# Nine z buffers, other operation estimates and a longer patience with ScalarE's tables, in a planned scan, attention and mixture kernel

## Chip, cores and metric

One core of a Trainium2 chip runs the whole kernel. The metric is the device time of one execution in microseconds, the median of several runs. The five engines are named as in the profile: PE (TensorE), DVE (VectorE), ACT (ScalarE), POOL (GpSimd) and SP (SyncE, which issues nearly all DMAs).

## What is computed

The input is `x` of shape (4, 384, 32, 32), all float32. The reference has two layers, cut here to what matters.

```python
# layer 0: group norm, then a selective scan in four directions
xs = cross_scan(gn(x))                                  # rows, columns, and both reversed
dts, Bs, Cs = split(einsum('bkdl,kcd->bkcl', xs, x_proj_weight), [12, 16, 16])
dt = softplus(einsum('bkrl,kdr->bkdl', dts, dt_projs_weight) + dt_projs_bias)
# per batch, direction, channel d and state n, along 1024 places:
h = h * exp(dt * A) + (dt * u) * B
y = sum over n of h * C
x = x + gelu(layernorm(cross_merge(y + D * u)))
# layer 1: per batch 1024 tokens of 384
t = t + attention(ln(t))          # 6 heads of 64, causal, 64 keys back
t = t + mixture(ln(t))            # 4 experts, the best 2 of each token, hidden size 1536, gelu
```

## The kernel before

**The scan.** One tile holds 128 rows of 1024 places: 32 channels by 4 of the 16 states. A block is 32 channels of one direction of one batch (192 blocks), and each has 4 such groups of states, so there are 768 scan slots. Two blocks make a pair whose slots alternate: slots 8p to 8p+7 belong to pair p, even slots to its first block and odd ones to its second (`place_of`). A slot is five steps.

- `times_b` (L808): POOL multiplies the spread dt*u (a dtu tile) by B into a z buffer. It may be up to three slots ahead of the scan (AHEAD, L547).
- `decay` (L824): ACT makes dA = exp(dt * A) from the spread dt (a dts tile) into one of two PSUM buffers.
- `scan` (L850): one DVE instruction runs the recurrence, in place in z or in dA.
- `times_c` (L837): the product by C, by POOL from z into z, or by DVE from dA into z. The choice is made in `scan` by the planned clocks of the two engines, and POOL is chosen only when z is three slots ahead.
- `fold_y` (L884): PE adds up the states by products with a constant matrix into a PSUM bank, two slots at a time. Then those two z buffers are free, and after four such steps DVE adds the bank to the earlier directions' sum, which SP loads from and stores to device memory.

`time_steps` makes dt and dt*u of a third of a direction (exp and ln on ACT, products on DVE) and writes them to device memory as dtr. `spread` (L798) loads them back, block by block and with every channel repeated four times, into the dts and dtu tiles; in the profile both loads are named dts<-dtr. A block's dtu tile is released after its fourth `times_b`, its dts tile after its fourth `decay`. `group_norm` (L618) prepares the next batch; from the z buffers it takes one for each yd tile and two at once for xo.

**The rest.** Attention of a batch (`tokens`) starts when the scan of that batch is folded. Then come its routing and its experts. Experts work in blocks of 128 rows, 19 per batch and 76 in all; a block has four chunks, each of which is a product into one PSUM bank (`hidden`, L1350), three gelu instructions on ACT (`gelus`, L1371) and a product into the output. Three banks (`banks`) serve folds, attention and `hidden` together. Eight weight buffers serve attention, which keeps four of them, and the experts.

**What sets the order.** Nothing of the order is written out by hand. Every part is a Python generator that yields the operation it wants next, and class `Machine` keeps a planned clock for each engine. An operation gets an estimated cost in `Engine.ask` (L154). `Machine.choose` (L322) takes, for each engine, an operation that is ready at the planned time, and the program's order on each engine is the order of these choices. On the chip every engine runs its list in that order and waits by semaphores, so an instruction that is not ready holds up all behind it. An estimate changes no instruction, only the order.

For ACT, `choose` prefers operations that need no other activation table than the loaded one. An operation of another table is taken when it has been ready for longer than PATIENCE, or when nothing else is ready. `settled` (L257) delays a request until its inputs are planned to be written by half a microsecond from now (SOON).

Of the kernel before, what the change touches and what calls it, by code (L numbers as in the profile page):

```python
# [17 lines left out]
P = 128  # L18
B, D, HH, WW = 4, 384, 32, 32
L = HH * WW  # L20
# [22 lines left out]
HID_RANK = 2  # L43
GELU_BIAS = EARLY
FAVOUR = 1.0
TILES, EPS, NZ = 3, 1e-5, 7
CORES = 1
NEG = -1.0e30

# [80 lines left out]
class Engine:  # L130
# [23 lines left out]
    def ask(self, op, a, k):  # L154
        aps = [v for v in list(a) + [v for n, v in k.items() if n not in ("out", "accum_out")] if hasattr(v, "tensor")]
        if "out" in k:
            outs, ins = [k["out"]], aps
        else:
            outs, ins = aps[:1], aps[1:]
        if op == "value_load":  # L160
            outs, ins = [], aps
        if op == "tensor_tensor_reduce":
            outs, ins = outs + ins[-1:], ins[:-1]
        if k.get("accum_out") is not None:
            outs = outs + [k["accum_out"]]
        for v in list(k.values()):
            if isinstance(v, bass.IndirectOffsetOnAxis):
                ins = ins + [v.ap]
        n = max(v.free_size() if callable(v.free_size) else v.free_size for v in (outs if op == "matmul" else outs + ins))
        size, table = 0, None  # L170
        if "dma" in op:
            size = max(_nbytes(v) for v in outs + ins[:1])
            if op == "indirect_dma_start":
                size = P * D * 4
            cost = dict(pool=1.0, act=0.38, sp=0.48)[self.name]
        elif self.name == "pe":
            cost = max(n, 122) * (0.00088 if op == "transpose" else 0.00176)
            if outs[0].shape[0] == 32:
                cost = 0.01 + 0.00022 * n
            if ins[0].shape[0] < 32:  # L180
                cost *= 0.6
        elif self.name == "act":
            cost = 0.08 + 0.00085 * n + 0.1 * sum(hasattr(k.get(v), "tensor") for v in ("bias", "scale"))
            cost += 0.19 if "accum_out" in k else 0.0
            table = TABLES.get(a[2]) if op == "activation" else None
        elif self.name == "pool":
            cost = 0.1 + 0.0022 * n
        elif self.name == "sp":
            cost = 1.5
        else:  # L190
            cost = 0.17 + 0.00198 * n if "scan" in op else 0.14 + 0.00105 * n
            if n < 256 and not any(v.space == PSUM for v in outs + ins):
                cost += 0.5
        asked = Op(self.name, outs, ins, cost, table, size)
        if self.name == "pe":
            asked.work = cost * min(ins[0].shape[0], P) / P if outs[0].shape[0] > 32 else 0.5 * cost
        return asked


def _nbytes(ap):  # L200
    n = 4
    for s in ap.shape:
        n *= s
    return n
# [6 lines left out]
class Machine:  # L211
# [42 lines left out]
            t = max(t, r + (HOP if e != eng else 0.0))  # L254
        return t

    def settled(self, *tiles):  # L257

        names = [ap.tensor.name for ap in tiles]
        return lambda: max(self.written.get(n, (0.0, None))[0] for n in names) <= self.t + SOON  # L260

    def account(self, op, start):
        e = op.eng
# [58 lines left out]
    def choose(self, eng):  # L322
# [4 lines left out]
        if eng == "act":  # L327

            same = [p for p in able if p[2].table in (None, self.table)]
            late = [p for p in able if p[2].table not in (None, self.table) and t0 - p[0] > PATIENCE]  # L330
            able = late or same or able
# [34 lines left out]
            raise RuntimeError("tracing is stuck")  # L366


PATIENCE = 3.0
SOON = 0.5  # L370
WINDOW, COLD = 3.413, 1.9
MARGIN, QUEUES = 1.0, ("sp",)

# [3 lines left out]
def conv_attn_hybrid(  # L377
# [89 lines left out]
    m = Machine(nc)  # L467
# [41 lines left out]
    work = ctx.enter_context(tc.tile_pool(name="work", bufs=1))  # L509
    rp = ctx.enter_context(tc.tile_pool(name="rp", bufs=2))  # L510
    zs_ = Stock(m, work, "z", NZ, [P, L])
    dtus, dts = (Stock(m, work, n, 4, [P, L]) for n in ("dtu", "dts"))
    bs_, cs_ = (Stock(m, work, n, 4, [P, L]) for n in ("rb", "rc"))
    rows = Stock(m, work, "row", NROW, [P, D])
    xbs, xbts, hss, ybs = (
# [38 lines left out]
    def place_of(s):  # L554

        return s // SP * 2 + s % 2, s % SP // 2
# [280 lines left out]
    def times_c(s, h, on_pool):  # L837
        n, g = place_of(s)
        i = blocks[n][0]
        yield lambda: (i, g, 1) in bcs  # L840
        if on_pool:
            yield from pool.tensor_tensor(zs[s], zs[s], bcs[i, g, 1], ALU.mult)
        else:
            yield from dve.tensor_tensor(zs[s], h, bcs[i, g, 1], ALU.mult)
            das_.give(h)
        if n % NB == NB - 1:
            cs_.give(bcs.pop((i, g, 1)))
        ready.add(s)

    def scan():  # L850

        for s in range(NSLOT):
            n, g = place_of(s)
            i = blocks[n][0]
            yield lambda: s in zs and s in das
            z, da = zs[s], das.pop(s)
            on_pool = count_of["times"] >= min(s + AHEAD, NSLOT) and m.clock["pool"] < m.clock["dve"] + LEAD
            h = z if on_pool else da
            if turns[i][1] >= 2:
                yield from dve.tensor_tensor_scan(  # L860
                    h[:, ::-1], da[:, ::-1], z[:, ::-1], 0.0, ALU.mult, ALU.add
                )
            else:
                yield from dve.tensor_tensor_scan(h, da, z, 0.0, ALU.mult, ALU.add)
            count_of["scan"] = s + 1
            if s % SP == 0:
                m.spawn(fold_y(n), EARLY)
            if on_pool:
                das_.give(da)
                m.spawn(times_c(s, h, True))  # L870
            else:
                yield from times_c(s, h, False)
        ended.append(True)
        yield lambda: len(das_.free) == 2
        for stock in (banks, ybank):
            stock.free.append(das_.free.pop(0))
        for stock, n in ((zs_, NZ), (dts, 4), (dtus, 4)):
            yield lambda: len(stock.free) == n
            rows.free += stock.free
            stock.free = []  # L880
# [3 lines left out]
    def fold_y(n):  # L884


        i, t, j = blocks[n]
        b, k = turns[i]
        rows_y = ydr[b][t, j : j + 2].rearrange("j r l -> (j r) l")
        prev = yield from yps.take("yp")  # L890
        yield from sp.dma_start(prev, rows_y)
        ps = None
        for g in range(NG):
            s = n // 2 * SP + 2 * g
            yield lambda: s in ready and s + 1 in ready
            pair = zs[s], zs[s + 1]
            yield m.settled(*pair)
            mm = Calls()
            if ps is None:
                ps = yield from banks.take("ps_y", 0)  # L900
            for n_z, z in enumerate(pair):
                for h in range(2):
                    if k % 2:
                        rhs = z.rearrange("p (w h) -> p w h", h=HH)[:, :, ts(h, HH // 2)]
                    else:
                        rhs = z[:, ts(h, LH)]
                    q = 32 * (2 * n_z + h)
                    mm.matmul(ps[q : q + 32, :], fold, rhs, start=g == 0, stop=g == NG - 1)
            yield from pe.all(mm)
            zs_.give(zs.pop(s), zs.pop(s + 1))  # L910
        yield from dve.tensor_tensor(prev, ps, prev, ALU.add)
        if k == LAST_BY_COLUMNS:
            yield from act.copy(
                ps.rearrange("p (h w) -> p w h", w=WW), prev.rearrange("p (w h) -> p w h", w=WW)
            )
            yield from act.copy(prev, ps)
        banks.give(ps)
        yield from sp.dma_start(rows_y, prev)
        yps.give(prev)
        folded[b] = folded.get(b, 0) + 2  # L920
        if folded[b] == KG * NB:
            have.add(("scan", b))
# [553 lines left out]
    with tc.manual_schedule():  # L1476
        for b in range(B):
            m.spawn(group_norm(b), EARLY)
        for gen in (turn_loads(), time_steps(), state_rows(0), state_rows(1), spread(1), spread(0)):
            m.spawn(gen, EARLY)  # L1480
        for gen in (decay(), times_b(), scan()):
            m.spawn(gen)
        m.spawn(layer1(), EARLY)
        for gen in (prepare(), mixture()):
            m.spawn(gen, LATER)
        m.run()
# [54 lines left out]
```

## Time and profile before

| | |
|---|---|
| runs | 4070.57, 4078.01, 4080.30 us; median 4078.01 |
| profiled execution | 4065.49 us, of it the span from first to last instruction 4063.8 |
| busy, of the span | PE 74%, DVE 71%, ACT 60%, POOL 70% |
| scan on DVE | 768 instructions, 2.276 to 2.288 us each on average |
| product by B on POOL | 768, 2.358 us each |
| product by C | 375 on POOL at 2.356 us, 393 on DVE at 1.221 us |
| dA on ACT | 768, 1.116 us each |
| activation tables | 388 loads, 1.283 us each |
| mean granted TensorE clock | 0.804 of full speed |

Times in the profile are microseconds unless marked ns. In a group of instructions, the numbers after the first bar are their busy time and the mean length of one in ns; those after the second bar are the idle time of the engine just before them, and what ended it. In a list of waits the numbers are the total, how many, and the longest. L141 and L152 are the two helper lines through which all planned operations go, so groups are told apart by the names of their tiles. [...]

### The profile page before, as it was taken

Reading aid. Unit: us, or ns where it says so; the run is one execution under the profiler, and the core shown is the slowest. Engines: PE = TensorE matmul, PEld = TensorE weight load, DVE = VectorE, ACT = ScalarE, POOL = GpSimd, SP = SyncE. Lnnn points to the kernel's source line nnn. Section 1 sums busy time; section 2 is a strip of 40 time slices with the busy share of each in tenths; the row PEclk is TensorE's granted clock in tenths of the full one; section 3 lists DMA queues with packets and bytes.
Section 4 is the critical chain, followed back from the end, with each engine's and each line's share of the span. In section 5 each row is a group of like instructions: output and inputs, shape, how many; then the busy total and the mean of one; then the engine's idle time right before and its main releaser. Section 6 shows DMA issues by size and latency. Waiting matters only on the chain. (4 is left out here: it accounts for less than half of the span.)

```text
span 4063.8 us, 49234 instructions
## 1 busy us (share of the span) xinstructions
PE 3014.8 (74%) x15856; PEld 1854.0 (46%) x15856; DVE 2878.0 (71%) x3064; ACT 2432.7 (60%) x3979; POOL 2855.7 (70%) x1490
## 2 busy tenths in 40 slices
PE   3554455576674888677777786767799999998998
PEld 1000000043441455445454444444466788887886
DVE  2999999998889888888888889888897232101001
ACT  3554455476774798777776787877777345222221
POOL 1999989989897789999987899899997110101001
PEclk8555566577775899878877787887799999998997
DMA  5565564634345989464668795664569754998995
GB/s 200 203 250 209 217 209 151 209 109 162 114 154 184 382 315 355 164 229 140 215 209 283 268 358 195 230 197 171 190 243 337 240 170 142 345 335 295 315 317 193
DMA packets 368570, 935.11 MB, mean 230 GB/s; under 512 B 48372, under 2 KB 160120, under 8 KB 368312
## 3 DMA queue, kind: packets, MB, share of 16 engines
q1 hardware_dynamic: 360120, 906.79, 63.6%
q0 software_dynamic: 8192, 25.17, 1.8%
q8 instruction: 126, 2.06, 0.2%
q14 instruction: 132, 1.08, 0.1%
HBM read 786.39 MB, written 164.30 MB: 234 GB/s over the span
## 5 line engine op out<-in xcount | busy, mean ns | idle before, releaser
L141 POOL TENSOR_TENSOR z<-dts,bc 128x1024 f32<-128x1024 f32 x768 | 1792.2, 2358 | 177.7 <-PE ps_y L152 95.3
L141 ACT ACTIVATE dA<-dts,a 128x1024 f32<-128x1024 f32 x768 | 851.1, 1116 | 485.5 <-DVE z L141 456.6
L152 PE MATMUL ps_y<-z,fold 128*32 128x512 f32 x3072 | 734.9, 806 | 536.1 <-POOL z L141 253.6
L141 DVE TENSOR_TENSOR_SCAN dA<-dA,z 128x1024 f32<-128x1024 f32 x393 | 899.1, 2288 | 107.6 <-ACT dA L141 88.6
L141 POOL TENSOR_TENSOR z<-z,bc 128x1024 f32<-128x1024 f32 x375 | 879.6, 2356 | 102.6 <-DVE z L141 99.7
L141 DVE TENSOR_TENSOR_SCAN z<-dA,z 128x1024 f32<-128x1024 f32 x375 | 843.8, 2276 | 41.2 <-ACT dA L141 39.4
L152 PEld LDWEIGHTS ps_hid<-xbt,w_sb 128*128 128x128 f32 x5472 | 682.1, 201 | 132.5 <-issue 25.7
L152 PE MATMUL ps_hid<-xbt,w_sb 128*128 128x128 f32 x5472 | 702.0, 286 | 38.0 <-ACT dt L141 19.4
L152 PE MATMUL y_ff<-w_sb,hs 128*128 128x384 f32 x1824 | 659.7, 500 | 19.2 <-ACT hs L141 15.2
L141 ACT ACTIVATE hs<-ps_hid,bb 128x128 f32<-128x128 f32 x912 | 270.5, 366 | 457.1 <-PE ps_hid L152 351.6
L152 PEld LDWEIGHTS ps_y<-z,fold 128*32 128x32 f32 x3072 | 95.1, 123 | 971.4 <-POOL z L141 466.2
L141 ACT ACT_TABLE_LOAD x388 | 497.8, 1283 | 17.2 <-issue 3.6
L141 DVE TENSOR_TENSOR z<-dA,bc 128x1024 f32<-128x1024 f32 x393 | 479.8, 1221 | 13.0
L152 PEld LDWEIGHTS y_ff<-w_sb,hs 128*128 128x128 f32 x1824 | 331.7, 195 | 240.5 <-issue 47.5
L141 POOL DMA_INDIRECT cb<-ysdr,idx x64 | 61.7, 963 | 441.6 <-issue 281.7
L141 DVE COPY xbt<-ps_xb 128x384 f32<-128x384 f32 x39 | 21.7, 556 | 407.7 <-PE ps_xb L152 407.7
L152 POOL TENSOR_TENSOR rn<-rn,half 128x1 f32<-128x1 f32 x96 | 52.5, 547 | 265.6 <-DVE rn L152 256.2
L141 POOL DMA_INDIRECT xsdr<-tks,idx x64 | 63.9, 999 | 168.9 <-DMA xsdr<-tks,idx 119.5
L152 PE MATMUL ps_dt<-xd,dtw_sb 12*128 12x512 f32 x192 | 99.8, 856 | 45.9 <-ACT dt L141 19.2
L152 PE MATMUL ps_o<-v,pt 128*128 128x64 f32 (+1 forms) x720 | 110.1, 315 | 19.6 <-DVE tt L141 7.2
L141 ACT COPY dt<-ps_sp 128x512 f32<-128x512 f32 x96 | 56.0, 584 | 113.5 <-DVE e L141 113.2
L152 PEld LDWEIGHTS ps_o<-v,pt 128*128 128x128 f32 (+1 forms) x720 | 104.9, 227 | 29.4 <-DVE tt L141 7.7
(189 smaller groups left out, 3219.4 us busy)
## 6 DMA issues: line engine op xcount, KB each, us to landing
w_sb<-wl SPq DMA_DIRECT2D x608, 576.0 KB
dts<-dtr SPq DMA_DIRECT2D x384, 512.0 KB
bc<-xdr SPq DMA_DIRECT2D x128, 512.0 KB
ub<-udr SPq DMA_DIRECT2D x48, 512.0 KB
dtr<-e SPq DMA_DIRECT2D x48, 512.0 KB
dtr<-dt SPq DMA_DIRECT2D x48, 512.0 KB
yp<-ydr SPq DMA_DIRECT2D x96, 256.0 KB
ydr<-yp SPq DMA_DIRECT2D x96, 256.0 KB
```

The lines of the kernel that those rows point to most:

```text
L141: return getattr(self.real, op)(*a, **k)
L152: getattr(self.real, op)(*a, **k)
```

## The change

Five things change; the instructions that compute are the same.

- There are nine z buffers, not seven, and three dtu and three dts buffers, not four of each. All are 128 x 1024 tiles, fifteen before and after.
- The estimates for folds, for products with fewer than 32 rows and for ACT are larger. The share of a fold's cost that counts for the planned clock of TensorE is larger too.
- PATIENCE is 5.0, not 3.0.
- The constant SOON is replaced by an argument of `settled`, whose default is -0.5.
- `fold_y` passes SURE, which is -0.5, as that argument.

```diff
-TILES, EPS, NZ = 3, 1e-5, 7
+TILES, EPS, NZ, SURE = 3, 1e-5, 9, -0.5
...
             if outs[0].shape[0] == 32:
-                cost = 0.01 + 0.00022 * n
+                cost = 0.02 + 0.0004 * n
             if ins[0].shape[0] < 32:
-                cost *= 0.6
+                cost *= 0.9
         elif self.name == "act":
-            cost = 0.08 + 0.00085 * n + 0.1 * sum(hasattr(k.get(v), "tensor") for v in ("bias", "scale"))
+            cost = 0.1 + 0.00088 * n + 0.1 * sum(hasattr(k.get(v), "tensor") for v in ("bias", "scale"))
...
-            asked.work = cost * min(ins[0].shape[0], P) / P if outs[0].shape[0] > 32 else 0.5 * cost
+            asked.work = cost * min(ins[0].shape[0], P) / P if outs[0].shape[0] > 32 else 0.7 * cost
...
-    def settled(self, *tiles):
+    def settled(self, *tiles, sure=-0.5):
...
-        return lambda: max(self.written.get(n, (0.0, None))[0] for n in names) <= self.t + SOON
+        return lambda: max(self.written.get(n, (0.0, None))[0] for n in names) <= self.t - sure
...
-PATIENCE = 3.0
-SOON = 0.5
+PATIENCE = 5.0
...
-    dtus, dts = (Stock(m, work, n, 4, [P, L]) for n in ("dtu", "dts"))
+    dtus, dts = (Stock(m, work, n, 3, [P, L]) for n in ("dtu", "dts"))
...
-        for stock, n in ((zs_, NZ), (dts, 4), (dtus, 4)):
+        for stock, n in ((zs_, NZ), (dts, 3), (dtus, 3)):
...
-            yield m.settled(*pair)
+            yield m.settled(*pair, sure=SURE)
```

## The prediction

> **What bounds the kernel now.** I read the page's 40 slices first (one slice is 101.6 us), then busy time by stretch, then the waits of each engine, then the groups.
>
> ```profile
> span 4063.8 us, 49234 instructions
> ...
> PE   3554455576674888677777786767799999998998
> ...
> DVE  2999999998889888888888889888897232101001
> ACT  3554455476774798777776787877777345222221
> POOL 1999989989897789999987899899997110101001
> ```
> For 31 slices DVE and POOL are at 8 to 9 tenths: the loop over 768 scan slots, from its first scan at 104 us to its last at 3140. For the rest PE alone is full. So the time is the loop's length plus the PE work left when the loop ends.
>
> ```profile
> 800.00:1300.00 500.00, 330.46 (x1638) 189.92 (x1638) 435.79 (x539) 330.05 (x559) 442.05 (x238) 0.70 0.41 142
> 1300.00:1600.00 300.00, 239.52 (x1337) 147.75 (x1337) 256.14 (x172) 251.38 (x341) 258.09 (x116) 0.89 0.92 345
> 1600.00:2200.00 600.00, 451.43 (x2393) 282.57 (x2392) 512.97 (x548) 458.43 (x731) 540.10 (x275) 0.82 0.61 208
> 3500.00:4064.00 564.00, 532.73 (x3185) 428.42 (x3183) 37.68 (x72) 130.61 (x413) 44.68 (x47) 0.94 0.86 301
> ```
> The columns are stretch, length, then busy us of PE, its weight loads, DVE, ACT, POOL, then clock, DMA share, GB/s. Summed over the six stretches that make up 800 to 3145, DVE is busy 2041 and POOL 2097 of 2345 us: idle 304 and 248. From 100 to 800 they idle only 26 and 39 of 700, so nothing is to be had there.
>
> The gelu groups count expert blocks (12 gelus each): 35 blocks run under the loop, 41 after it. At 3800 to 4000, 150 gelus are 12.5 blocks: **16 us a block** in the tail. Under the loop the pace is 98 gelus in 1400 to 1600, 4.1 blocks per 100 us, while no attention runs, and 75 in 1600 to 2200 and 84 in 2400 to 3000, 1.1 per 100 us, while it does.
>
> ```profile
> POOL z L141 <- DVE z L141: 99.7, 44, 13.3
> POOL z L141 <- PE ps_y L152: 95.3, 50, 10.0
> ...
> DVE dA L141 <- ACT dA L141: 88.6, 68, 3.8
> ...
> DVE z L141 <- ACT dA L141: 39.4, 35, 3.6
> ...
> DVE dA L141 <- POOL z L141: 12.5, 9, 6.3
> ```
> These are us in total, times, longest. POOL waits for a z buffer that a fold on PE must free (95.3), yet DVE hardly waits for POOL (12.5): its waits are for ScalarE's dA (128.0).
>
> **The change, part by part.** The scheduler is a model run while the program is written; its costs alter only the order on each engine.
>
> *Nine z buffers.* A fold frees two every two slots. Two slots are 2 x 3.96 us (3036 us / 767 steps) = 7.9 us, so two more buffers cover a fold that is late by 7.9 us; the 50 waits average 1.9 us, the longest is 10.0. I take the whole 95.3 us, and 10.0 us of waits on xdr<-xo (xo holds z buffers), off POOL: 105 us. It shortens the loop only if the order then gives POOL more products by C. One moved product costs POOL 2.356 us and saves DVE 1.221, so w us freed on POOL give w x 1.221/3.577 = 0.341 w: **-36 us**. Ends: 0 (DVE waited 12.5 in all) and -105. What is late next on POOL is the product by C behind its scan (99.7) and the spread loads.
>
> *Three dtu and three dts buffers.* Blocks go in pairs. With three buffers, the pair's second block waits until the pair before has finished its first: released at slot 6, needed at slot 9. In this trace that gap is 4.6 to 17.4 us on POOL (5th to 90th percentile, median 10.2) and 6.8 to 15.3 on ACT (median 10.0). A load's landing, read as its semaphore's last update before that semaphore's next use, comes 3.3 to 12.5 us after issue (median 4.9) and up to 16.7 after the release. Laid against each other pair by pair, 10 of 93 loads come late for POOL by 31 us in all and 7 for ACT by 13. POOL's converts as above, ACT's in full: 31 x 0.341 + 13 = 24. What hides it is the lead of z (median 6.0 us before its scan) and of dA (2.0): I take half, **+12 us**. Ends: 0, and 44 if every gap shrank to its lower quartile (6.9 and 8.1: 60 and 23 us late). SP issues at the same releases as before, so nothing queued behind these loads moves.
>
> The Trainium skill, "DMA: Bandwidth & Descriptors", section "Anatomy of one DMA — SWDGE (gpsimd) path", gives about 2.0 us plus bytes/436e9 for the GpSimd path. As an estimate for 512 KB that is 3.2 us, and no load would be late; this trace's quickest load agrees at 3.3, its median of 4.9 does not, and the sum goes by the trace.
>
> *PATIENCE 3 to 5.*
>
> ```profile
> L141 ACT ACTIVATE dA<-dts,a 128x1024 f32<-128x1024 f32 x768 | 851.1, 1116 | 485.5 <-DVE z L141 456.6
> ...
> L141 ACT ACT_TABLE_LOAD x388 | 497.8, 1283 | 17.2 <-issue 3.6
> ```
> 388 loads at 1.283 us, 368 of them before 3145. But `choose` waits only if an operation of the loaded table, or of none, is ready; an idle ScalarE changes tables at once, and it idles 485.5 us before dA. In the trace 112 stretches under the loop hold only expert gelus; 80 of them hold one chunk. I take a tenth of 368 away: 37 loads, 47 us of ScalarE. DVE waited 92.6 us for a dA with a load just before it, so a tenth is **-9 us**. Ends: -93 and +93, since longer gelu stretches delay a dA too. The other side: a ps_hid chunk can hold one of three PSUM banks 2 us longer. I take half a block lost to the tail, +8 us (ends: 0 and +94, worked out below).
>
> ```profile
> 2605.01 0.47 ACT L141 COPY yb<-y_ff 128x384 f32<-128x384 f32 x1
> ...
> 2605.51 1.28 ACT L141 ACT_TABLE_LOAD   x1
> ...
> 2606.80 0.37 ACT L141 ACTIVATE hs<-ps_hid,bb 128x128 f32<-128x128 f32 x1
> ```
> The load follows the copy by 0.03 us and the gelu follows the load by 0.01. The Trainium skill, "ScalarE: Activation LUTs", section "What ACT_TABLE_LOAD costs", adds a drain of about 1380 ns, 2.66 us a switch. At that price 37 loads would be 98 us of ScalarE instead of 47; this trace shows no drain, so 1.283 is used.
>
> *Estimates.* A fold product goes from 0.123 to 0.225 us warm; the trace has 734.9 us for 1536 calls (two of the 3072 records each), 0.478. A 12-row time-step product goes from 0.541 to 0.811 (99.8 us for 96 calls, 1.040). An exp goes from 1.050 to 1.101 (trace 1.116), a gelu from 0.289 to 0.313 (0.366). PE was planned too fast and its folds came late. What a truer order can touch is POOL's 99.7 us behind scans (x 0.341 = 34) and DVE's waits on PE from 800 to 3145, 106.7: 141. I take a third, **-48 us**; ends -141 and +141, for a new order can also be a worse one.
>
> *SURE.* -0.5 makes `t - sure` the old `t + 0.5`: nothing.
>
> **The sum.** Loop: -36 + 12 - 9 - 48 = -81 us. A shorter loop leaves more expert blocks to the tail: between 81 x 0.011 x 16 = 14 and 81 x 0.041 x 16 = 53 us; middle 34. With the half block: -81 + 34 + 8 = -39. The profiled execution took 4065.5 us (span 4063.8), so 4026.5 by it; the median of the three runs shown, 4078.0, is 12.5 above it, so **4039**.
>
> **The rivals.** *More.* Half the idle of DVE and POOL goes (276 / 2 = 138 us), tail given back at the middle rate (0.42): -80, 3998. For it: both engines idle 11 to 13%. Against it: DVE's waits are scattered over many small causes.
>
> *Nothing.* The z waits were harmless (DVE waited 12.5 us), the loads go on as before since ScalarE is idle when it switches, and late spreads cost 12 x 0.58 = 7: 4085.
>
> *Slower.* Longer-held PSUM banks starve the experts. In 1300 to 1600, 2200 to 2400 and 3000 to 3145 (645 us) 21.9 blocks run, a chunk each 7.4 us; at 2 us more it is 69 chunks instead of 88, 4.7 blocks or 76 us of tail, and 1.1 blocks, 18 us, more in the attention stretches: 94. Against a net loop gain of 47: +47, 4125. It decides from about 3 lost blocks (47 / 16). For it: a fold keeps one bank throughout. Against it: patience only counts while exp work is queued.
>
> **How the numbers follow.** The smallest difference a measurement can tell is about 0.3%, 12 us. Forecast 4039 (its own range 3998 to 4066): 0.40. More: 0.18. Nothing: 0.14. Slower: 0.28. Faster is 0.58. Range 3960 to 4135: down past the second case, since the ends of the order term allow it, up past the slower one.
>
> **What would show it.** Right: POOL's waits on ps_y near 0; the last scan near 3060; 43 blocks after it; 340 to 360 table loads; few POOL or ACT waits on dts<-dtr. Wrong: waits on dts<-dtr over 60 us (late spreads); 45 or more blocks after the loop at an unchanged loop (banks); loads still near 388 and loop unchanged (nothing); more waits of DVE on PE or ACT than 107 and 128 (a worse order).

## The result, and the profile after

The changed kernel takes 4105.72 us (median of four runs, 4102.83 to 4107.63) and the kernel before 4074.29 us beside it (4065.28 to 4080.30). The ratio is 1.0077, with a 95% interval from 1.0063 to 1.0090: slower by 31 us. The profiled execution took 4107.63 us, of it a span of 4105.9.

First the 40 slices of the changed kernel (one is now 102.6 us), and the groups of the product by B and of the table loads.

```profile
span 4105.9 us, 49117 instructions
...
PE   3544444467766497777777778777899999998998
...
DVE  2999999999898888998988688999882233101001
ACT  3545455477675588777777687777772344222221
POOL 1999989999998899999987899999991110001001
...
L141 POOL TENSOR_TENSOR z<-dts,bc 128x1024 f32<-128x1024 f32 x768 | 1794.0, 2359 | 127.3 <-DMA dts<-dtr 88.3
...
L141 ACT ACT_TABLE_LOAD x338 | 433.7, 1283 | 15.4 <-PE ps_hid L152 4.8
```
DVE and POOL leave the high digits about one slice earlier, and 50 of the 388 table loads are gone. In the waits of POOL and DVE (total, times, longest), the wait for a fold fell from 95.3 to 34.4 us. A wait for late spread loads came in its place; 68.8 of its 88.3 us are the very first load, which was 67.3 of 69.4 before, so the other loads rose from 2.1 to 19.5 us. ScalarE too now waits for a spread load before a dA, 10 times and 27.5 us in all, where in the kernel before it never did.

```profile
POOL z L141 <- DMA dts<-dtr: 88.3, 9, 68.8
POOL z L141 <- DVE z L141: 67.0, 32, 8.6
...
POOL z L141 <- PE ps_y L152: 34.4, 6, 17.1
...
DVE dA L141 <- ACT dA L141: 83.9, 56, 6.3
...
DVE z L141 <- ACT dA L141: 38.6, 29, 3.4
```
The loop's last scan ends at 3082 us, 58 earlier than in the kernel before. Yet the span is 42 longer, so the stretch after the loop grew by 100. Two answers of the windows view, for the instructions on the hs tiles alone, show why. The ACT column counts gelus, 12 to a block. This is the kernel before, cut at its loop's end:

```profile
800.00:3140.00 2340.00, 310.08 (x831) 154.92 (x832) 125.26 (x420) 0.81 0.64 226
3140.00:4064.00 924.00, 349.65 (x995) 176.78 (x993) 145.24 (x493) 0.96 0.76 262
```
And this is the changed one, cut at its own:

```profile
800.00:3082.00 2282.00, 269.21 (x711) 133.84 (x712) 105.77 (x357) 0.79 0.63 219
3082.00:4106.00 1024.00, 393.88 (x1114) 198.79 (x1112) 164.25 (x555) 0.96 0.77 269
```
Of the 912 gelus, 493 fell after the loop before (41.0 blocks) and 555 do now (46.2). At 16 us a block, 5.2 blocks are 83 of the 100 us. So the loop became shorter, by 58 us where 81 were forecast, and the tail took back 83 us where 42 (34 + 8) were forecast.

### The profile page after: what moved, and what is told of

It reads as the page before. It is cut to its first block, busy times and chain, and to the rows that moved or that the text cites. A ratio compares the mean times of both kernels' runs of the same rounds, so it can differ in the third digit from the quotient of the medians.

```text
span 4105.9 us, 49117 instructions
## 1 busy us (share of the span) xinstructions
PE 3060.7 (75%) x15868; PEld 1885.7 (46%) x15868; DVE 2884.5 (70%) x3062; ACT 2359.8 (57%) x3914; POOL 2884.8 (70%) x1503
## 5 line engine op out<-in xcount | busy, mean ns | idle before, releaser
L141 POOL TENSOR_TENSOR z<-dts,bc 128x1024 f32<-128x1024 f32 x768 | 1794.0, 2359 | 127.3 <-DMA dts<-dtr 88.3
L141 POOL TENSOR_TENSOR z<-z,bc 128x1024 f32<-128x1024 f32 x388 | 911.9, 2357 | 74.9 <-DVE z L141 67.0
L141 DVE TENSOR_TENSOR_SCAN dA<-dA,z 128x1024 f32<-128x1024 f32 x380 | 869.3, 2288 | 95.3 <-ACT dA L141 83.9
L141 DVE TENSOR_TENSOR_SCAN z<-dA,z 128x1024 f32<-128x1024 f32 x388 | 872.4, 2276 | 47.0 <-ACT dA L141 38.6
L141 DVE TENSOR_TENSOR z<-dA,bc 128x1024 f32<-128x1024 f32 x380 | 464.0, 1221 | 11.1
L152 PE MATMUL ps_s<-k,q 64*128 64x192 f32 (+1 forms) x384 | 101.5, 408 | 53.3 <-ACT dt L141 27.5
L141 DVE COPY yb<-y_ff 128x384 f32<-128x384 f32 x29 | 16.0, 553 | 177.0 <-PE y_ff L152 146.6
```

Source lines behind the costliest of these rows:

```text
L141: return getattr(self.real, op)(*a, **k)
L152: getattr(self.real, op)(*a, **k)
```

## Experiments

Three theories were put against each other. **A**: the larger estimates cost the time. **B**: the longer patience does, by way of the PSUM banks. **C**: any new order moves the time by some tens of microseconds, and what was measured is mostly that. Times are medians; the kernel before, run beside each group, gave 4073.8 to 4079.8. Blocks left are expert blocks whose gelus come after the last scan, and the loop's end is the end of that scan, both from the profiled execution of each run.

### The parts alone

**e1, the buffers alone.**

```diff
-TILES, EPS, NZ = 3, 1e-5, 7
+TILES, EPS, NZ = 3, 1e-5, 9
...
-    dtus, dts = (Stock(m, work, n, 4, [P, L]) for n in ("dtu", "dts"))
+    dtus, dts = (Stock(m, work, n, 3, [P, L]) for n in ("dtu", "dts"))
```


> The kernel before with nine z and three dtu and dts buffers alone. Theory A (the larger estimates cost the time: with them the order gives attention and the experts less of PE under the loop, and 5 blocks of 16 us more are left for the tail): this run lacks them, the loop is 30 to 60 us shorter, at most 2 blocks more than 41 are left, 10 to 35 us faster than before. Theory B (patience: a chunk's gelus hold a PSUM bank longer): the same as A here. Theory C (any new order moves the time by some tens of us, and no part has an effect of its own): anywhere within 30 us of before. Late spread loads would show as over 60 us of waits on dts<-dtr and no gain.

Measured: 4090.8 us, ratio 1.0022 (1.0009 to 1.0036). The loop ends at 3136, 42.8 blocks are left, 347 table loads. POOL's waits for folds fall to 7.0 us, and its waits for spread loads behind the very first are 25.2. Neither A's gain nor the 60 us of late loads.

**e2, the patience alone.**

```diff
-PATIENCE = 3.0
+PATIENCE = 5.0
```


> The kernel before with PATIENCE 5 alone. Theory A: table loads fall to 340 to 370, blocks left after the loop stay within 1.5 of 41, time between 30 us faster and 10 slower. Theory B: 44 or more blocks are left after the loop, 30 to 90 us slower than before. Theory C: within 30 us of before, loads alone follow the setting.

Measured: 4089.5 us, ratio 1.0026 (1.0012 to 1.0041), 358 loads, 41.2 blocks left. B finds no support here: no block is lost. In the trace a chunk's first gelu under the loop starts 1.6 us after its last product on average, and 1.7 before, so the banks are not held longer.

**e3, the estimates alone.**

```diff
-                cost = 0.01 + 0.00022 * n
+                cost = 0.02 + 0.0004 * n
...
-                cost *= 0.6
+                cost *= 0.9
...
-            cost = 0.08 + 0.00085 * n + 0.1 * sum(hasattr(k.get(v), "tensor") for v in ("bias", "scale"))
+            cost = 0.1 + 0.00088 * n + 0.1 * sum(hasattr(k.get(v), "tensor") for v in ("bias", "scale"))
...
-            asked.work = cost * min(ins[0].shape[0], P) / P if outs[0].shape[0] > 32 else 0.5 * cost
+            asked.work = cost * min(ins[0].shape[0], P) / P if outs[0].shape[0] > 32 else 0.7 * cost
```


> The kernel before with the new estimates alone (folds, 12-row products, ScalarE). Theory A: attention of the first three batches takes longer by tens of us each, 45 to 49 blocks are left after the loop instead of 41, 50 to 120 us slower than before. Theory B: no block is lost, within 20 us of before. Theory C: within 30 us of before.

Measured: 4147.5 us, ratio 1.0163 (1.0142 to 1.0184). The loop ends at 3078, and 48.8 blocks are left.

**e4, buffers and patience, no estimates** (the edits of e1 and e2).

> The change without its estimates: nine z buffers and PATIENCE 5. Theory A: keeps the shorter loop (3075 to 3110) and loses at most 2 blocks, 15 to 60 us faster than before and 45 to 90 faster than the whole change. Theory B: still 44 or more blocks left, slower than before by 10 to 50. Theory C: within 30 us of before.

Measured: 4036.3 us, ratio 0.9887 (0.9867 to 0.9908), faster than both kernels. The same windows as above, for e4:

```profile
800.00:3094.00 2294.00, 288.62 (x798) 142.86 (x798) 118.75 (x405) 0.80 0.65 228
3094.00:4034.00 940.00, 362.22 (x1026) 182.75 (x1026) 149.82 (x507) 0.96 0.77 264
```
The loop is 47 us shorter than before, and only 507 gelus (42.2 blocks) are left. With or without buffers and patience the estimates cost about 70 us (4147.5 against the 4079.8 of the kernel before beside it, 4105.7 against 4036.3). That fits A. But against the same 4079.8 buffers and patience lose 11 and 10 us alone and gain 44 together, which no sum of effects gives. So C had to be measured.

### What chance in the order is worth

HOP is the planned time of a handover between engines. Two thousandths of a microsecond mean nothing, but they decide near ties another way, and every later choice may follow.

```diff
-HOP = 0.15
+HOP = 0.148
```
Likewise 0.149, 0.151 and 0.152. For the kernel before:

> The kernel before with the planned handover at 0.148 instead of 0.150 us, nothing else. Theory A: within 25 us of 4074. Theory C: 30 us or more away from it.

> The kernel before with the planned handover at 0.152 instead of 0.150 us. One tie moved the kernel before from 4074 to 4130. Theory C (the order's luck is some 30 us either way, and the order of the kernel before was a lucky one): between 4070 and 4140, likely above 4074. Theory A: within 25 us of 4074.

> The kernel before with the planned handover at 0.149. If its order at 0.150 is a lucky one: 4090 to 4140. If the two high ones were the unlucky ones: 4060 to 4085.

> The kernel before with the planned handover at 0.151. Lucky at 0.150: 4090 to 4140. Otherwise: 4060 to 4085.

For e4:

> Nine z buffers and PATIENCE 5, with the planned time of a handover between engines changed from 0.150 to 0.152 us, which means nothing and only decides near ties another way. It measures what chance in the order is worth. Theory A: within 25 us of 4036 and below 4074. Theory C: 30 us or more away, as far as the parts of the change seem to move it.

> Nine z buffers and PATIENCE 5 without the new estimates, handover 0.148. Theory C: between 4030 and 4110, likely near 4060, the middle of the two orders of it so far (4036 and 4076). Theory A: below 4074.

For the whole change:

> The whole change with the handover at 0.148. Theory A (the estimates cost some 65 us whatever the order): 4090 to 4150. Theory C (the change itself is worth nothing either way): between 4050 and 4140 with no tie to 4106.

> The whole change with the handover at 0.152. Theory A: 4090 to 4150. Theory C: between 4050 and 4140.

Measured, with the mean over the orders and the standard deviation of one order:

| handover | 0.148 | 0.149 | 0.150 | 0.151 | 0.152 | mean | deviation |
|---|---|---|---|---|---|---|---|
| kernel before | 4129.8 | 4081.4 | 4074.3 | 4111.4 | 4128.6 | 4105 | 26 |
| buffers and patience | 4043.2 | | 4036.3 | | 4076.3 | 4052 | 21 |
| whole change | 4114.7 | | 4105.7 | | 4118.6 | 4113 | 7 |

A meaningless tie moves the kernel before by up to 56 us. Its own order is the luckiest of the five, 31 us below their mean, though the one at 0.149 is only 7 us above it: of the last two expectations, if the order is a lucky one, 0.151 fell inside the range and 0.149 below it. The whole change is 8 us above that mean, with a standard error (how far off such a difference of means may well be) of 12 (26 / root 5 and 7 / root 3, as root of the sum of squares): on the average over orders no difference is shown. Between the rows the parts do stand out. Buffers and patience together are worth -53 (error 17), and all three orders lie below every one of the kernel before but one (4076.3 against 4074.3). The estimates then cost +61 (error 13). So A and C are both right, about different things. The windows of the third order of the whole change (handover 0.152), cut at its loop's end, are like those of the first:

```profile
800.00:3071.00 2271.00, 251.56 (x660) 124.67 (x660) 99.74 (x336) 0.79 0.62 216
3071.00:4119.00 1048.00, 413.00 (x1164) 208.62 (x1164) 170.56 (x576) 0.95 0.78 271
```
576 gelus are 48.0 blocks. The three orders of the change leave 46.2, 47.8 and 48.0; those of e4 leave 42.2, 42.8 and 42.1; the five of the kernel before 46.2, 41.0, 41.0, 44.0 and 43.0.

### Which of the estimates

e5, e13 and e14 are e4 with the fold's cost and its share alone, e6, e15 and e16 are e4 with ScalarE's cost alone, each at three handover values (0.150, 0.148, 0.152).

```diff
-                cost = 0.01 + 0.00022 * n
+                cost = 0.02 + 0.0004 * n
...
-            asked.work = cost * min(ins[0].shape[0], P) / P if outs[0].shape[0] > 32 else 0.5 * cost
+            asked.work = cost * min(ins[0].shape[0], P) / P if outs[0].shape[0] > 32 else 0.7 * cost
```


> Nine z buffers and PATIENCE 5 (4036 us) plus only the larger cost and TensorE share of a fold. Theory A1 (the fold's cost is what takes planned PE time from attention and experts): 44 to 46 blocks are left after the loop instead of 42, 4060 to 4100 us. Theory A2 (ScalarE's estimates do it): within 15 us of 4036. Theory C (any new order moves the time by some tens of us): anywhere from 4010 to 4080.

> Nine z buffers, PATIENCE 5 and the fold's larger cost and share, handover 0.148. If the fold's cost takes the time (mean of the three orders without estimates 4052, with them 4113): 4075 to 4110, 44 or more blocks after the loop. If ScalarE's estimates do: 4035 to 4075, 42 to 43 blocks.

> The same at handover 0.152. Fold's cost: 4075 to 4120, 44 or more blocks. ScalarE's estimates: 4035 to 4080, 42 to 43 blocks.

Measured: 4084.1, 4072.8 and 4076.3, mean 4078: +26 over e4's orders, with an error of about 13; 44.4, 44.1 and 44.8 blocks left.

```diff
-            cost = 0.08 + 0.00085 * n + 0.1 * sum(hasattr(k.get(v), "tensor") for v in ("bias", "scale"))
+            cost = 0.1 + 0.00088 * n + 0.1 * sum(hasattr(k.get(v), "tensor") for v in ("bias", "scale"))
```


> Nine z buffers and PATIENCE 5 (4036 us) plus only ScalarE's larger estimates. Theory A1: within 15 us of 4036. Theory A2: 4060 to 4100, attention of the first three batches longer by 20 us or more each. Theory C: anywhere from 4010 to 4080.

> Nine z buffers, PATIENCE 5 and ScalarE's larger estimates, handover 0.148. ScalarE's estimates: 4075 to 4115. Fold's cost: 4035 to 4075. Half each: both pairs of runs between 4060 and 4095.

> The same at handover 0.152. ScalarE's estimates: 4075 to 4120. Fold's cost: 4035 to 4080.

Measured: 4091.8, 4104.6 and 4108.5, mean 4102: +50, with an error of about 13; 44.0, 45.0 and 44.0 blocks left, the loop's end at 3114, 3110 and 3119 (e4's orders: 3094, 3087, 3122). ScalarE's estimates cost the larger part. The fold's cost brings the blocks it was expected to cost, but its time is only twice its error: likely, not settled. The third estimate, of products with fewer than 32 rows, has no run of its own; 26 + 50 is 76 against 61 for all three, less than the errors apart.

## Why the prediction was wrong

**What bounds the time.** Loop plus the PE work left was the right frame. Over the 20 profiles (two kernels and 18 variants) the spans lie between 4033 and 4147 us, and the loop's end plus 16 us for each block left lies below the span by 262 to 293 us in every one (mean 276, standard deviation 9). Its correlation with the span is 0.97 (1 is in step, 0 no relation). The loop's end alone does not carry the time: its correlation with the span is 0.06, because a shorter loop comes with more blocks left (correlation of the two -0.73). The prediction tied the blocks left to the loop's length, 0.42 us of tail for each us of loop, and but for half a block to nothing else.

Attention is part of it. The start of the last batch's attention goes with the span at 0.70. In the changed kernel it first loads its tokens at 3211 us, 129 after the loop (3174 and 34 in the kernel before), because attention goes batch by batch and the third batch's routing is worked out only at 3129. From that start to the end it is 895 us, and 890 in the kernel before.

**Nine z buffers, fewer spread buffers, patience.** Right in size together, and for the buffers in mechanism. The three terms were -36 + 12 - 9 = -33 for the loop; the loops of e4's three orders end at 3101 on the average, those of the five orders before at 3140: -39 (error 14). POOL's waits for folds are 94 to 121 us in the five orders before and 3 to 8 in e4's three, and POOL takes 377 to 396 products by C instead of 362 to 375. In the changed kernel the late spread loads cost POOL about 17 us (31 forecast) and ScalarE 27.5 (13 forecast). Table loads fell to 338 (340 to 360 forecast), but they are no proof of the patience: the five orders before have between 358 and 391, and e1 has 347 with the old patience. In their one order each, buffers alone end the loop at 3136 and patience alone at 3143, against 3140, so the split of the -33 is not shown.

**The blocks given back.** 34 + 8 us were too much for these parts: e4's orders leave 42.4 blocks on the average, those before 43.0, with an error of 1.0. The loop's -39 and 0.7 blocks fewer at 16 us are -50, close to the measured -53.

**Estimates: the step that failed.** "What a truer order can touch ... I take a third, -48 us". Measured +61 on the mean of three orders. The term priced the estimates by the waits of the loop alone and put what a new order does to the experts at nothing, beyond the give-back for a shorter loop. The loop did get shorter: from 3101 in e4's orders to 3074 in those of the change, -27 (error 11). But the blocks left rose from 42.4 to 47.3. These 5.0 blocks (error 0.6) are 80 us at 16 us each, so the two make +53 of the +61. For the fold's cost alone the same reckoning gives -11 + 33 = +22 (26 measured), and for ScalarE's +13.6 + 31.6 = +45 (50 measured). So each of the two leaves about two more blocks; what each does to the loop is no more than its error of about 11. That the estimates push blocks out of the loop is shown. Why they do is in part argued, from two observations.

First, ScalarE's new estimates are not truer. The prediction compared them with the records' mean lengths (a gelu 0.366, an exp 1.116 us). The time for which the engine is taken runs from one start to the next. Here are ScalarE's merged rows of the kernel before, with start, length, and how many are merged:

```profile
2633.96 0.88 ACT L141 ACTIVATE hs<-ps_hid,bb 128x128 f32<-128x128 f32 x3 [0.37 <-PE ps_hid L152]
...
2636.16 2.15 ACT L141 ACTIVATE dA<-dts,a 128x1024 f32<-128x1024 f32 x2
```
Three gelus of 0.366 take 0.88, not 1.10. From start to start, where nothing idles between, the median is 0.265 us for a gelu and 1.055 for an exp. The old estimates were 0.289 and 1.050, the new ones 0.313 and 1.101: the change moved them away from what the engine does. The fold's new 0.225 is closer than the old 0.123, since in a quick row of the stretch shown below sixteen records (two a call) take 1.92 us, 0.24 a call, and in slower rows more; it gained nothing either. No run lowered ScalarE's estimates, so whether their being untrue or only their size costs the time stays open.

Second, a larger cost leaves less room in the plan, and the experts, which come last in priority, can be placed later; that is read from the code. On the chip the first expert gelu came at 1343 us before (1329 to 1351 over its five orders) and at 1422, 1397 and 1359 in the three orders of the change. The first batch's last gelu is at 2400, 2360 and 2353 instead of 2281 (2281 to 2338 over the five orders before). By then the third batch's attention has begun, or is about to (2372, 2361, 2383), and the `combine` of the first batch falls into it: all eight of its tiles in each of the three, three to seven in the orders before, counted by the start of a tile's gathers. That attention takes 757, 749 and 711 us up to the end of its routing's arithmetic, against a mean of 685 over the five orders before; over the 20 profiles its length goes with the number of combine tiles in it (correlation 0.7). This does not explain all: with ScalarE's estimates alone the first batch's last gelu is at 2282 to 2295, no later than before, and the third batch's attention still takes 746, 700 and 733 us.

What this looks like on PE, in the changed kernel, with the third tile of that attention: its turned scores, the input of its next product (ps_o), are copied at 2617.1, and that product starts at 2680.3.

```profile
2616.41 2.27 PE L152 MATMUL ps_hid<-xbt,w_sb 128*128 128x128 f32 x18
2618.62 1.92 PE L152 MATMUL ps_y<-z,fold 128*32 128x512 f32 x16
...
2653.73 1.92 PE L152 MATMUL ps_y<-z,fold 128*32 128x512 f32 x4 [5.00 <-POOL z L141]
2655.58 1.65 PE L152 MATMUL ps_c<-ident,cb 128*128 128x128 f32 x6
...
2680.25 1.97 PE L152 MATMUL ps_o<-v,pt 128*128 128x64 f32 x8 [2.30 <-ACT dt L141]
```
PE works through folds, expert products and a combine (ps_c) ahead of it in its list, and stands idle for a late z on the way. Only one tile at a time may be in this part of attention, so the next ones wait too. Over the 24 tiles of the first three batches such waits sum to 300 us, and to 105 in the kernel before. Both are extremes: the other two orders of the change have 200 and 231, the other four before 131 to 181. A likely reason is the `rows` stock: a combine tile asks for four of its ten buffers at once, and attention must take one before ps_o can be asked for. That is read from the code; no kernel with more rows or another combine was run.

**The sum.** -53 for buffers and patience and +61 for the estimates make +8 between means. The order of the kernel before lay 31 below its mean and that of the change 7 below its own: 8 + 31 - 7 = 32, the 31 measured but for rounding, as it must be. What it says is where the 31 us lie: about 8, with an error of 12, in the change, and the rest in the luck of two single orders. **Rivals.** The slower one named the right sign and the lost blocks, but the wrong cause: with the longer patience alone no block is lost, nor in e4's orders. That the result came so near its 4125 is luck. And the case that no one of them named is that the kernel's own order was a lucky one: the ends of the order term, 141 either way, stood for it, but the forecast itself gave a new order no loss.

## What to carry to other kernels

Where a planner makes the order, measure first what a meaningless tie is worth, and compare means over a few orders: here one order is worth 26 us (0.6%), so two single orders that differ by 0.8% tell little of a change. Before calling an estimate truer, compare it with the time from start to start, not with the mean length of the records, and expect even a truer cost to shift who comes last. When a stage becomes shorter, count the work that it pushes into the next one: here the estimates took 27 us off the loop and put 80 behind it.

## What the runs showed of the hardware

ScalarE starts the next operation before the record of the last has ended: 0.366 us of record and 0.265 from start to start for a gelu of 128 columns, 1.116 and 1.055 for an exp of 1024. The Trainium skill, "ScalarE: Activation LUTs", section "What ACT_TABLE_LOAD costs", says that back-to-back ACTIVATEs overlap by about 93 ns; the trace's 101 and 61 ns stand on both sides of that.
